# Expert mixtures: the second tile of a switch arm fetched inside the arm, and a code hint for the arm

## The chip, the cores and the metric

The kernel runs on one core of a Trainium2 chip. Its time is the device time of one execution in microseconds (us), the median of several runs. A core has five engines, each with an instruction queue of its own: PE (matrix products), DVE (vector), ACT (activations), POOL (here above all indirect DMAs and small tensor work) and SP (here the issuer of plain DMAs). They wait for each other through semaphores.

## The reference

The kernel computes twelve layers of a network on 1024 tokens of 256 numbers, float32 throughout: four groups (L0 to L3) of a cross-attention, an attention and a feed-forward layer. Three of the feed-forward layers, L0, L2 and L3, are mixtures of eight experts: a gate picks two experts per token (one in L2), and the token's output is the sum of the chosen experts' outputs, weighted by the gate. L3's in short:

```python
logits = x_flat @ router_w.T
probs = jax.nn.softmax(logits, axis=-1)
top_v, top_i = jax.lax.top_k(probs, K)             # K = 2 of E = 8
top_v = top_v / jnp.sum(top_v, axis=-1, keepdims=True)
...
h = jax.nn.gelu(jnp.einsum('ech,ehf->ecf', expert_in, w1), approximate=False)
y = jnp.einsum('ecf,efh->ech', h, w2)
...
out = out + tok * (gate * keep.astype(x.dtype))[:, None]
```

L2 has the same shape with biases and one expert per token; L0 has a gated hidden layer (silu(x W1) times x W2, then W3) of 682 units.

## The kernel before

The layers run one after the other. The change touches only the three mixtures, which share the function `experts` (L1647 to L1727).

Tokens are sorted by expert into tiles of 128 rows; a tile belongs to one expert. How many tiles each expert needs depends on the data. `slots` (L1571 to L1645) works this out on DVE, POOL and PE: `rows` (L1600, where each tile's expert lies in the weight table), `used` (L1602, how many tiles there are), then, by a chain over L1605, L1607, V (L1616 to L1624) and matmuls with R, `token` (L1642, the token of each row of each tile) and `share` (L1644, its gate). With 23 tiles at most in L0 and L3 and 15 in L2, `sure = tiles - 7` of them (16, 8, 16) are there whatever the data. These are written out straight. The remaining 0 to 7 are the business of a switch: `count`, the value of `used`, is loaded into a register of each engine, and each engine branches to the arm written for this number of further tiles. At the head of each arm an instruction hints at the branch out of it; the branch into it has no hint.

A tile i (`tile`, L1692) is:

- `fetch` (L1655): SP loads the expert's row from `rest` (a copy of `rows`) into a register and issues two DMAs, the first and second layer's weights, into one of three buffers W;
- `gather` (L1664): POOL fetches the tile's 128 token rows by an indirect DMA, xs;
- `turn` (L1672): PE transposes xs (`pst`), DVE or ACT in turn copy it to xT;
- `hidden`: PE multiplies with the first layer (`p` in L0, `psh` in L2 and L3, both under the helper's line L199), ACT and DVE apply the activation to hT;
- `pso`: PE multiplies with the second layer, DVE scales with the gate into y (L1705), and POOL adds y into the output in memory with an indirect scatter (L1706). Each scatter waits until the one before it has landed.

The order within a tile is fixed: fetch and gather of tile i+2, hidden of i, turn of i+1, pso of i. The straight tiles run with `end = sure + 2`, so that tile `sure - 1` still fetches and gathers for tile `sure + 1`, the second tile of whichever arm comes:

```python
        for i in range(sure):
            tile(i, sure + 2)
        held = dict(W), list(xs), list(xT)
        for n in self.tc.Switch(count - sure, E):
```

What is held across the switch (two tiles' weights, one tile's rows and one transposed tile) belongs to every arm, and its buffers are not used again within an arm. So one weight buffer of the three is left for an arm's third and further tiles. `self.fixed` pins the order of PE's instructions and a few others as written; what is not pinned, the loads of registers among them, is placed by a scheduler.

Of the kernel before, what the change touches and what calls it, by code (L numbers as in the profile page):

```python
# [27 lines left out]
E = 8  # L28
# [148 lines left out]
class Net:  # L177
# [1469 lines left out]
    def experts(self, name, xin, slots, weights, width, cols, tiles, wp, sp, pst, pso, hidden):  # L1647

        nc = self.nc
        rows, token, share, used = slots  # L1650
        total = self.dram.tile([NTOK + SPARE, D], F32, tag=f"{name}o", name=f"{name}o")
        nc.sync.dma_start(total[:NTOK, :].rearrange("(t p) d -> p t d", p=P), self.x)
        nc.sync.dma_start(total[NTOK:, :], xin[NTOK:, :])

        def fetch(i, rows):  # L1655
            W = wp.tile([P, width], F32, tag="W", name="W", bufs=3)
            r = nc.values_load(
                rows[0:1, i : i + 1], [mybir.EngineType.SP], min_val=0, max_val=(E - 1) * P
            )
            for o in (slice(0, cols), slice(cols, width)):  # L1660
                nc.sync.dma_start(W[:, o], self.io[weights][bass.ds(r, P), o])
            return W

        def gather(i):  # L1664
            xs = sp.tile([P, D], F32, tag="xs", name="xs", bufs=3)
            nc.gpsimd.indirect_dma_start(
                xs, None, xin, bass.IndirectOffsetOnAxis(token[:, i : i + 1], 0),
                bounds_check=NTOK + SPARE - 1,
            )
            return xs  # L1670

        def turn(xs):  # L1672
            ps = self.psum(pst, [P, 2, P], "pst")
            for kc in range(2):
                self.tr(ps[:, kc, :], xs[:, kc * P : (kc + 1) * P])
            xT = sp.tile([P, 2, P], F32, tag="xT", name="xT")
            self.evac(xT, ps)
            return xT

        self.fixed = True  # L1680

        W, xs = {0: fetch(0, rows)}, [gather(0), gather(1)]
        rest = sp.tile([P, tiles], U32, tag="rest", name="rest", bufs=1)
        self.pinned(nc.gpsimd.tensor_copy(rest, rows))
        W[1] = fetch(1, rest)

        sure = tiles - (E - 1)
        count = nc.values_load(used[0:1, 0:1], min_val=sure, max_val=tiles)
        self.warm(7)
        xT = [turn(xs.pop(0))]  # L1690

        def tile(i, end):  # L1692
            if i + 2 < end:
                W[i + 2] = fetch(i + 2, rest)
                xs.append(gather(i + 2))
            hT = hidden(W[i], xT.pop())
            if i + 1 < end:
                xT.append(turn(xs.pop(0)))
            n = hT.shape[1]
            W2 = W.pop(i)[:, cols : cols + n * D].rearrange("p (c n) -> p c n", n=D)  # L1700
            po = self.psum(pso, [P, D], "pso")
            for c in range(n):
                self.mm(po, hT[:, c, :], W2[:, c, :], c == 0, c == n - 1)
            y = sp.tile([P, D], F32, tag="y", name="y")
            nc.vector.tensor_scalar(y, po, share[:, i : i + 1], None, ALU.mult)  # L1705
            nc.gpsimd.indirect_dma_start(  # L1706
                total, bass.IndirectOffsetOnAxis(token[:, i : i + 1], 0), y, None,
                bounds_check=NTOK + SPARE - 1, compute_op=ALU.add,
            )

        for i in range(sure):
            tile(i, sure + 2)
        held = dict(W), list(xs), list(xT)
        for n in self.tc.Switch(count - sure, E):
            W, xs, xT = dict(held[0]), list(held[1]), list(held[2])
            for i in range(sure, sure + n):
                tile(i, sure + n)
        if name != "l3":
            self.warm(14)
        self.fixed = False  # L1720
        for t in range(0, NT, 2):
            nc.sync.dma_start(
                self.x[:, t : t + 2, :],
                total[t * P : (t + 2) * P, :].rearrange("(t p) d -> p t d", p=P),
            )
        if name != "l3":
            self.ready_all()  # L1727
# [842 lines left out]
```

## Time and profile before

| what | us |
|---|---|
| median of 3 runs (lowest to highest) | 3158.01 (3157.7 to 3166.25) |
| the profiled execution, its own time | 3158.53 |
| its span, first to last instruction | 3156.8 |
| L0's tiles: first hidden matmul to the last y | 641.27 to 801.98 |
| L2's tiles | 2394.16 to 2480.52 |
| L3's tiles | 2981.68 to 3142.36 |

The mean granted clock of PE over the span is 0.974 of full speed. In the profiled execution 19, 11 and 20 tiles were in use, so the arms for 3, 3 and 4 further tiles ran.

A row of the timeline gives the start and the busy time of one or several like instructions, the engine, the line, the operation with what it writes and reads, and in brackets how long the engine had been idle before it and which event ended that. Lines such as L199 belong to helpers, so that the tile's name tells what is done. An indirect DMA on POOL shows the time that POOL needs to issue it, not its transfer. Loads of registers, branches and hints are in no row; they show as idle time.

### The profile page before, as it was taken

How to read it: one execution, taken by the hardware profiler on the slowest of the kernel's cores; microseconds unless marked ns; L12 is line 12 of the kernel's file. 1: busy time of each engine (PE TensorE's matmuls, PEld its weight loads, DVE VectorE, ACT ScalarE, POOL GpSimd, SP SyncE). 2: the span in 40 equal slices, each digit the busy share in tenths (PEclk: the TensorE clock that was granted, in tenths of full speed). 3: DMA queues.
4: the chain of work that ended last, by engine and by line, in shares of the span. 5: the costliest groups of instructions: out<-in, count | busy, mean ns of one | idle time of the engine just before them, and what ended most of it. 6: DMA issues, size and time to landing. Idle time of an engine off the chain costs nothing.

```text
span 3156.8 us, 66834 instructions
## 1 busy us (share of the span) xinstructions
PE 2972.9 (94%) x28271; PEld 2215.7 (70%) x28271; DVE 1244.5 (39%) x3346; ACT 1354.2 (43%) x2691; POOL 336.0 (11%) x495
## 2 busy tenths in 40 slices
PE   7999998899899999999998999999999888889896
PEld 5666665699566666666676767777768767678796
DVE  5888885422344444444446512112142100145200
ACT  5888885311233333333333522222242477753211
POOL 1000001232100000000002100000022211111132
PEclk9999999899999999999999999999999899998898
DMA  6343341198112121212149111111117355510395
GB/s 224 115 140 122 112 137 64 58 330 296 34 49 72 55 84 44 82 46 80 55 136 297 35 42 63 42 63 42 63 50 274 109 190 190 179 40 3 138 335 181
DMA packets 174620, 368.52 MB, mean 117 GB/s; under 512 B 12614, under 2 KB 141646, under 8 KB 163726
## 3 DMA queue, kind: packets, MB, share of 16 engines
q1 hardware_dynamic: 163390, 348.78, 32.3%
q0 software_dynamic: 9600, 13.11, 2.1%
q8 instruction: 230, 3.77, 0.5%
q10 hardware_dynamic: 1280, 1.88, 0.2%
q14 instruction: 120, 0.98, 0.1%
HBM read 349.45 MB, written 14.68 MB: 115 GB/s over the span
## 4 chain that ended last, share of the span: by engine, by line
PE 77%; DMA 8%; issue 4%; DVE 4%; ACT 3%; POOL 1%; SPq 0%; POOLq 0%; DVEq 0%; ACTq 0%
PE acc L199 18%; PE pss L199 16%; PE pst L199 14%; PE pst L203 7%; PE psk L199 6%; DMA l3o<-y,token 4%; PE pso L199 4%; PE ps L199 3%; PE s L199 3%; PE p L199 3%; DMA l0o<-y,token 1%; DMA xs<-l2i,token 1%; PE py L199 1%; PE po L199 1%; PE psh L199 1%
## 5 line engine op out<-in xcount | busy, mean ns | idle before, releaser
L199 PE MATMUL acc<-ctx,st 128*128 128x257 f32 (+1 forms) x1664 | 397.2, 383 | 0.0
L199 PE MATMUL pss<-qk,ctxT 128*128 128x512 f32 (+1 forms) x832 | 391.5, 596 | 0.7 <-DVE qk L678 0.7
L199 PEld LDWEIGHTS acc<-ctx,st 128*128 128x128 f32 (+1 forms) x1664 | 310.2, 190 | 94.5 <-issue 36.1
L504 DVE CUSTOM_DVE_ANT_0 Sx<-s,mneg 128x384 f32<-128x384 f32 (+1 forms) x512 | 264.2, 570 | 88.1 <-PE s L199 88.1
L694 DVE TENSOR_TENSOR top<-pss,top 128x512 f32<-128x512 f32 x192 | 132.7, 691 | 403.6 <-ACT st L689 403.5
L203 PE MATMUL pst<-cst,Sx 128*128 128x128 f32 (+1 forms) x1736 | 251.6, 283 | 16.3 <-ACT aT L1280 8.6
L718 ACT ACTIVATE st<-st 128x512 f32<-128x512 f32 (+1 forms) x208 | 130.6, 629 | 294.5 <-DVE st L717 294.5
L990 ACT ACTIVATE Pr<-pss 128x512 f32<-128x512 f32 (+1 forms) x512 | 219.9, 524 | 59.5 <-PE pss L199 58.0
L548 ACT ACTIVATE PT<-pst 128x384 f32<-128x384 f32 x512 | 215.1, 489 | 63.1 <-PE pst L203 62.0
L199 PEld LDWEIGHTS pss<-qk,ctxT 128*128 128x128 f32 (+1 forms) x832 | 155.3, 187 | 122.4 <-issue 105.7
L203 PEld LDWEIGHTS pst<-cst,Sx 128*128 128x128 f32 (+1 forms) x1736 | 186.1, 141 | 62.4 <-ACT PT L548 27.7
L689 ACT COPY st<-pss 128x512 f32<-128x512 f32 (+1 forms) x208 | 121.5, 584 | 203.5 <-PE pss L199 203.5
L199 PE MATMUL pst<-wst,ctxT 128*128 128x256 f32 (+1 forms) x832 | 183.4, 380 | 0.0
L199 PE MATMUL psk<-ctxT,wst 128*128 128x512 f32 (+1 forms) x512 | 181.8, 513 | 0.8 <-ACT qT L852 0.8
L318 POOL TENSOR_TENSOR rs<-mv,cst 128x1 f32<-128x1 f32 x80 | 17.4, 217 | 1449.8 <-DVE mv L314 1420.1
L199 PEld LDWEIGHTS pst<-wst,ctxT 128*128 128x128 f32 (+1 forms) x832 | 153.5, 186 | 25.9 <-issue 2.7
L199 PE MATMUL pso<-W,hT 128*128 128x256 f32 x724 | 164.5, 379 | 0.0
L199 PE MATMUL pss<-q,ctxT 32*128 32x128 f32 (+1 forms) x3328 | 147.5, 293 | 16.6 <-issue 13.4
L199 PEld LDWEIGHTS psk<-ctxT,wst 128*128 128x128 f32 x512 | 88.3, 190 | 93.7 <-issue 92.1
L892 DVE TENSOR_TENSOR v<-pst,bvec 128x512 f32<-128x512 f32 (+1 forms) x112 | 73.1, 653 | 204.4 <-PE pst L199 204.4
L523 ACT ACTIVATE Sx<-Sx,neg 128x384 f32<-128x384 f32 (+1 forms) x256 | 145.8, 621 | 11.5 <-DVE neg L514 11.4
L199 PEld LDWEIGHTS pss<-q,ctxT 32*128 32x128 f32 (+1 forms) x3328 | 116.0, 188 | 47.7 <-issue 38.1
(404 smaller groups left out, 4427.1 us busy)
## 6 DMA issues: line engine op xcount, KB each, us to landing
ctxT<-in_ctxT_dram SPq DMA_DIRECT2D x64, 1601.0 KB
W<-in_L_experts_dram SPq DMA_DIRECT2D x51, 1024.0 KB
ctx<-in_ctx_dram SPq DMA_DIRECT2D x32, 1536.0 KB
W<-in_L_experts_dram SPq DMA_DIRECT2D x19, 1536.0 KB
ctx<-in_ctx_ones_dram SPq DMA_DIRECT2D x16, 1632.0 KB
ctx<-in_ctx_one_dram SPq DMA_DIRECT2D x16, 1542.0 KB
W<-in_L_experts_dram SPq DMA_DIRECT2D x19, 768.0 KB
W<-in_L_experts_dram SPq DMA_DIRECT2D x11, 1028.0 KB
```

The lines of the kernel that those rows point to most:

```text
L199: self.pinned(self.nc.tensor.matmul(out, lhsT, rhs, start=start, stop=stop))
L203: self.pinned(self.nc.tensor.transpose(out, in_, self.ident[:n, :n]))
L318: nc.gpsimd.tensor_tensor(rs[:, 0:1], mv[:, 1:2], self.c("eps"), ALU.add)
L504: self.pinned(nc.vector.tensor_tensor_reduce(out=Sx[:, j, :n], in0=ps[j][:, :n], in1=st["mneg"][:, o : o + n], op0=ALU.add, op1=ALU.max, s ...
L523: self.pinned(nc.scalar.activation(Sj[j], Sj[j], AF.Identity, bias=st["neg"][:, j - 2 : j - 1]))
L548: self.pinned(nc.scalar.activation(PT, ps, AF.Exp))
L689: pin(nc.scalar.copy(st[:kn], ps[:kn]))
L694: pin(nc.vector.tensor_tensor(top[b][:kn], ps[:kn], top[b][:kn], ALU.max))
L718: pin(nc.scalar.activation(st, st, AF.Exp, scale=HD**-0.5))
L892: nc.vector.tensor_tensor(o, ps[:kn, :n, :], bv[:kn].to_broadcast([kn, n, D]), ALU.add)
L990: nc.scalar.activation(st["Pr"][:kn, g : g + n, j, :], ps[j][:kn, :n, :], AF.Silu)
```

## The change

The straight tiles now run with `end = sure + 1`: the last of them fetches nothing, and weights and rows of tile `sure + 1` are asked for at the head of each arm that has at least two tiles, by the new function `ahead`. Across the switch one tile's weights and its transposed rows are held. Second, the loaded count less `sure` is put into a dictionary of one register expression per engine (`arm`), a hint for the switch is written after tile `sure - 3`, and the switch takes the same dictionary and the hint's label. The hint is not pinned: in the changed program the scheduler places the register load, the target's arithmetic and the hint ahead of the first tile of a stage, on DVE between L1605 and L1607, on POOL ahead of L1620, on ACT ahead of the first xT. On PE the load stays where it was and the hint follows just ahead of the first `pst` (in L2 somewhat earlier). On SP they stand ahead of the first fetch, in L2 after the fetch of tile 7. On POOL the gather of tile `sure + 1` now follows the scatter of tile `sure - 1`, in the arm; before, it preceded the last three scatters.

```diff
--- before.py
+++ after.py
@@ -1687,14 +1687,20 @@
         sure = tiles - (E - 1)
         count = nc.values_load(used[0:1, 0:1], min_val=sure, max_val=tiles)
         self.warm(7)
+        arm = {e: count - sure for e in count.engines} if hasattr(count, "engines") else {
+            e: count - sure for e in self.nc.engines
+        }
         xT = [turn(xs.pop(0))]
+
+        def ahead(i):
+            W[i] = fetch(i, rest)
+            xs.append(gather(i))
 
         def tile(i, end):
             if i + 2 < end:
-                W[i + 2] = fetch(i + 2, rest)
-                xs.append(gather(i + 2))
+                ahead(i + 2)
             hT = hidden(W[i], xT.pop())
-            if i + 1 < end:
+            if xs:
                 xT.append(turn(xs.pop(0)))
             n = hT.shape[1]
             W2 = W.pop(i)[:, cols : cols + n * D].rearrange("p (c n) -> p c n", n=D)
@@ -1709,10 +1715,14 @@
             )
 
         for i in range(sure):
-            tile(i, sure + 2)
+            tile(i, sure + 1)
+            if i == sure - 3:
+                self.tc.switch_hint(arm, E, label=name)
         held = dict(W), list(xs), list(xT)
-        for n in self.tc.Switch(count - sure, E):
+        for n in self.tc.Switch(arm, E, hint=name):
             W, xs, xT = dict(held[0]), list(held[1]), list(held[2])
+            if n > 1:
+                ahead(sure + 1)
             for i in range(sure, sure + n):
                 tile(i, sure + n)
         if name != "l3":
```

## The prediction

> **What bounds the kernel now.** The page comes first. Its chain that ended last puts 77% of the span on TensorE (PE), and the tiles of the three expert stages follow each other on PE at 8.17 us (L0), 7.25 us (L2) and 7.24 us (L3).
>
> ```profile
> PE 77%; DMA 8%; issue 4%; DVE 4%; ACT 3%; POOL 1%; SPq 0%; POOLq 0%; DVEq 0%; ACTq 0%
> ```
>
> So the change is worth what it takes from or adds to PE's idle time around the three switches. I read these in the timeline, 40 us at each switch. The tiles used were 19, 11 and 20, of which 16, 8 and 16 are sure, so the arms taken are n = 3, 3 and 4. L0:
>
> ```profile
> 774.50 0.48 DVE L1705 TENSOR_SCALAR y<-pso,share 128x256 f32<-128x256 f32 x1 [2.18 <-PE pso L199]
> 776.94 5.60 PE L199 MATMUL p<-xT,W 128*128 128x128 f32 x48 [2.48 <-SPq L1714]
> 777.90 1.55 POOL L1706 DMA_INDIRECT l0o<-y,token  x1 [4.82 <-DMA l0o<-y,token]
> 787.15 1.08 POOL L1666 DMA_INDIRECT xs<-l0i,token  x1 [7.69 <-PE p L199]
> ...
> 802.04 1.13 PE L199 MATMUL pso<-cst 128*128 128x256 f32 x4 [0.58 <-DVE y L1705]
> ```
>
> PE idles 2.48 us on entering the arm. On leaving it (last line), where a hint stands at the head of the arm, it idles 0.58 us, for DVE's y. POOL issues the last sure tile's scatter at 777.90, held by the scatter before, and its first gather of the arm 7.69 us after that scatter ends. L2 and L3:
>
> ```profile
> 2453.77 0.48 DVE L1705 TENSOR_SCALAR y<-pso,share 128x256 f32<-128x256 f32 x1 [6.76 <-PE pso L199]
> 2456.62 3.81 PE L199 MATMUL psh<-xT,W 128*128 128x128 f32 x32 [2.90 <-issue]
> 2458.55 1.55 POOL L1706 DMA_INDIRECT l2o<-y,token  x1 [6.27 <-DMA l2o<-y,token]
> 2466.18 1.09 POOL L1666 DMA_INDIRECT xs<-l2i,token  x1 [6.08 <-PE psh L199]
> 2469.11 0.41 PE L203 MATMUL pst<-cst,xs 128*128 128x128 f32 x2 [1.43 <-DMA xs<-l2i,token]
> ```
> ```profile
> 3103.04 5.44 PE L199 MATMUL psh<-xT,W 128*128 128x128 f32 x32 [4.04 <-issue]
> 3103.23 1.55 POOL L1706 DMA_INDIRECT l3o<-y,token  x1 [6.25 <-DMA l3o<-y,token]
> 3110.55 1.08 POOL L1666 DMA_INDIRECT xs<-l3i,token  x1 [5.77 <-DMA xs<-l3i,token]
> 3131.74 6.65 PE L199 MATMUL psh<-xT,W 128*128 128x128 f32 x32 [5.10 <-DMA W<-in_L_experts_dram]
> ```
>
> The same pattern, and in L3 one wait more: the fourth tile of the arm waits 5.10 us for its weights, because tiles 18 and 19 are fetched into one buffer. After the two long gaps of L3 the 32 hidden matmuls take 5.44 and 6.65 us instead of 3.73. The table of windows says why: the granted clock (third number from the end of a row) fell there, not after L2's 2.90 us gap.
>
> ```profile
> 2454.00:2473.00 19.00, 14.95 (x102) 13.99 (x103) 1.16 (x3) 4.82 (x17) 4.21 (x3) 1.00 0.54 158
> 3099.00:3112.00 13.00, 8.96 (x51) 8.58 (x52) 0.48 (x1) 1.46 (x3) 2.63 (x2) 0.87 0.60 192
> 3127.00:3142.00 15.00, 10.10 (x48) 9.37 (x48) 0.28 (x2) 1.19 (x2) 1.56 (x1) 0.77 0.45 152
> ```
>
> How long a gather takes from issue to landing is in the answer for the tile xs (least, median, most):
>
> ```profile
> DMA to landing us min/median/max: 2.9/4.7/7.0
> ```
>
> **The change part by part.** Losses before, to be set off. L0: gap 2.48. L2: gap 2.90, and the tile from 2463.94 to 2472.81 is 8.87 instead of 7.25 for the late gather: 1.62; 4.5 together. L3: gap 4.04, slow matmuls 1.71, weight wait 5.10, slow matmuls 2.92: 13.8.
>
> *The weights.* The fetch of tile `sure+1` moves from the last sure tile into the arm. It waits for the buffer of tile `sure-2`. SP has nothing between the fetch of tile `sure` (issued one tile, 7.2 to 8.2 us, earlier) and the arm, so even an unhinted entry of 6 us is hidden and it costs 0. The cover gone, it would be late microsecond for microsecond. Two buffers now serve within the arm: the weights of L3's tile 19 go where tile 17's were and start a tile earlier. Their first half takes 5.1 us (the wait above), tile 18 takes 7.24: the 5.10 and the 2.92 behind it go. L0 and L2 with n = 3 never had this wait.
>
> *The hint on PE.* The entry gap of 2.48, 2.90 and 4.04 becomes at most what the hinted exit shows, 0.58; I take 0.4.
>
> *The gather of tile `sure+1`*, moved with the weights, decides. Before, POOL issued it two tiles ahead, three scatters before the switch. Now it is in the arm, and on POOL's queue it stands behind the scatters of the last three sure tiles and the branch. The last of these is issued 2.9 to 4.3 us after its y, because each scatter waits for the one before to land. PE runs in order: it needs this gather for `pst`, ahead of the first arm tile's `pso`. PE reaches `pst` at the end of the last sure tile (774.46, 2453.73, 3099.00) plus 0.4 plus the hidden matmuls (5.35, 3.57, 3.57): 780.2, 2457.7, 3103.0. POOL ends the scatter at 779.45, 2460.10, 3104.78. Between neighbouring DMAs it idles 0.30; with branch and register work I take 0.8: gather issued at 780.25, 2460.9, 3105.6. Landing takes 2.9 (queue empty) to 4.7 (median, right behind a scatter). The Trainium skill, "DMA: Bandwidth & Descriptors", section "Queues, rings and completion order", says that a DMA engine takes turns between queues but consumes one queue's ring in order (it says so of hardware-made descriptors; POOL's share one queue too). By that rule the gather cannot pass the scatter issued 2.4 us earlier, and 4.7 is nearer; I take 4.2. The empty-queue row alone would make the sum about 4 us less. Landing: 784.5, 2465.1, 3109.8. Stalls of PE: 4.3, 7.4, 6.8 us.
>
> *The clock after these stalls.* Gaps of 2.48 and 2.90 left it full; 4.04 and 5.10 cost 1.71 and 2.92. The skill's "TensorE: Matmul & The Clock Gate", Part 1, gives a free-running window of about 3.4 us idle to slow and as long busy to recover, at half rate: up to 1.7 us a stall, and it speaks against this change. By the rule the three stalls would cost up to 5.1; by the rows I take 1.0 (L0, just past the edge), 2.5, 2.5: 6.0.
>
> *Early register loads.* The hint needs the tile count on every engine, so its load goes, with the target's arithmetic and the hint, from in front of the switch up into `slots` (all three stay ahead of the first tile on PE, ACT, DVE and POOL, not three tiles before the arm; on SP too, but for L2). ACT and POOL wait 17 us and 15 to 19 us there: 0. On PE the load stood there already. On SP it delays the first weights by some 0.2 us; PE waits then for the first xT: 0. If POOL's load ran past V's input, each stage would pay the excess, up to 1 us. On DVE it lies in the chain to `token`, right after L1605. No row has it; SP's load of `rows` bounds it above: written at 2968.96, DMA issued at 2970.08, 1.1 us with the issue. Below, 0.1, since it overlaps L1605. I take 0.4 a stage, 1.2 in all.
>
> Sum: L0 0.4+4.3+1.0-2.5 = +3.2; L2 0.4+7.4+2.5-4.5 = +5.8; L3 0.4+6.8+2.5-13.8 = -4.1; loads +1.2; together +6. The profiled execution took 3158.5 us (span 3156.8), 0.5 above the median of 3158.0, so 3164.
>
> **The rivals.**
> *Slower: POOL still pays for the arm's code.* From the scatter's end to the first gather POOL spent 7.70, 6.08 and 5.77 us. Less some 1 us for the load that moves away, 6.7, 5.1, 4.8 stay if the hint does not bring in POOL's code (it stands a stage ahead, and is not what PE's exit row tests). The gather then lands alone, 2.9 later: 789.1, 2468.1, 3112.5, which is 4.6, 3.0 and 2.7 later than above, plus some 1.5 for L0's clock: +18, 3176. It decides once POOL's entry takes over about 2 us, the lead that the scatter's landing gives anyway. For it: POOL's gaps are the longest of all engines. Against: the hinted exit on PE.
> *No change: the gather does not queue behind the scatter* and lands in 2.9: stalls 2.9, 6.1, 5.5, clock 0, 1.7, 1.7: 0.8+3.7-6.2+1.2, about 0: 3158. For it: the scatter's data are half landed by then. Against: the median of 4.7.
> *Faster: the gather is in time.* Only the gaps and L3's weights count: -2.1-4.1-13.4+1.2 = -18, 3140. It needs the last scatter about 5 us earlier in all three stages, and the rows show it held by the scatter before.
> *The change does nothing to entry*: if no hint works, PE's gap stays but hides under the gather, which is the first rival again.
>
> **How the numbers follow.** About 0.3% (9.5 us) is what a measurement of this kernel tells from no change. My forecast (3159 to 3170) has 0.58, its upper tail beyond 9.5 us a quarter of that; the slow rival 0.27, nearly all beyond; no change 0.10; faster 0.05. Slower: 0.15+0.26, about 0.41; faster 0.05; the same 0.54. Range: from 4 us below, for the early landing and a cheap load, to 20 above, for the slow rival: 3154 to 3178. The likeliest case's own range is 3159 to 3170.
>
> **What would show it.** In the changed profile's chain of waits: PE `pst` waits for DMA xs after the first hidden matmuls of each arm, 3 to 8 us; PE's entry gap under 0.6; no wait for W in L3's arm; in the timeline POOL's first gather of each arm within 1 us of the scatter's end (5 or more means the slow rival); the granted clock below 1 after the stalls in L2 and L3; DVE idle 0.3 to 0.6 between L1605 and L1607. I am wrong if PE meets no gather wait in the arms, or if L3's W wait is still there.

## The result and the profile after

The changed kernel takes 3174.74 us (median of 15 runs, 3166.69 to 3180.4), against 3157.72 of the kernel before in runs on the same chip (15 runs, 3151.49 to 3171.17). The two medians are 17 us apart; the ratio as it was estimated from all these runs is 1.0038, 95% interval 1.0026 to 1.005: slower by 0.38%, or 12 us, more than the 0.3% that a measurement of this kernel can tell from no change. The profiled execution took 3171.95 us, with a span of 3170.2 (3156.8 before) and a mean granted clock of 0.968 (0.974).

The page's chain that ended last is of no use this time. It follows POOL's scatters back into L3's arm and stops there; the line by engines reads

```profile
DMA 1%; issue 0%; POOL 0%; POOLq 0%
```

where that of before ran through the whole span. So I go to the timeline at once, with the same stretches as before. First L0's switch. The columns are start, busy time, engine, line, operation, and in brackets the engine's idle time before and what ended it.

```profile
778.68 5.52 PE L199 MATMUL p<-xT,W 128*128 128x128 f32 x48
778.88 0.48 DVE L1711 TENSOR_SCALAR y<-pso,share 128x256 f32<-128x256 f32 x1 [2.18 <-PE pso L199]
...
781.03 1.55 POOL L1712 DMA_INDIRECT l0o<-y,token  x1 [6.22 <-DMA l0o<-y,token]
...
783.03 1.09 POOL L1666 DMA_INDIRECT xs<-l0i,token  x1 [0.46 <-PE p L199]
...
789.12 0.69 PE L203 MATMUL pst<-cst,xs 128*128 128x128 f32 x2 [4.91 <-DMA xs<-l0i,token]
789.60 5.04 PE L199 MATMUL pso<-W,hT 128*128 128x256 f32 x12
...
811.33 0.92 PE L199 MATMUL pso<-cst 128*128 128x256 f32 x3 [0.58 <-DVE y L1711]
```

TensorE (PE) enters the arm without a gap: the first line has no bracket, where before it had 2.48. POOL issues its first gather 0.46 us after the scatter. But PE then stands 4.91 us before the transpose of that gather's rows, and the `pso` behind it takes 5.04 us instead of 2.76. L2, then L3:

```profile
2469.26 1.55 POOL L1712 DMA_INDIRECT l2o<-y,token  x1 [7.24 <-issue]
2471.44 1.09 POOL L1666 DMA_INDIRECT xs<-l2i,token  x1 [0.63 <-issue]
...
2475.76 0.66 PE L203 MATMUL pst<-cst,xs 128*128 128x128 f32 x2 [8.27 <-DMA xs<-l2i,token]
...
2476.21 5.69 PE L199 MATMUL pso<-W,hT 128*128 128x256 f32 x16
```
```profile
3118.30 1.55 POOL L1712 DMA_INDIRECT l3o<-y,token  x1 [5.89 <-issue]
...
3124.76 1.09 POOL L1666 DMA_INDIRECT xs<-l3i,token  x1 [4.91 <-DMA l3o<-y,token]
...
3127.66 0.69 PE L203 MATMUL pst<-cst,xs 128*128 128x128 f32 x2 [7.90 <-DMA xs<-l3i,token]
...
3128.14 5.70 PE L199 MATMUL pso<-W,hT 128*128 128x256 f32 x16
...
3133.68 3.73 PE L199 MATMUL psh<-xT,W 128*128 128x128 f32 x32
```

The same stall, 8.27 and 7.90 us, and after it 5.7 us for sixteen `pso` matmuls that take 3.62 at full clock. The table of windows shows the granted clock (third number from the end) down in all three places, L0, L2 and L3:

```profile
779.00:794.00 15.00, 10.09 (x60) 9.00 (x59) 1.48 (x3) 1.35 (x3) 3.69 (x3) 0.78 0.55 188
2470.00:2482.00 12.00, 6.24 (x21) 5.25 (x22) 0.00 (x1) 0.37 (x1) 2.95 (x3) 0.57 0.31 94
3120.00:3134.00 14.00, 6.34 (x21) 5.32 (x22) 0.07 (x1) 0.77 (x2) 3.16 (x3) 0.63 0.42 126
```

In L3 the fourth tile's wait for its weights (5.10 us before) is gone. All that was foreseen. What was not is in L0's `slots`, 150 us ahead of the switch:

```profile
627.76 0.29 DVE L1605 TENSOR_TENSOR place<-place,oh 128x128 f32<-128x128 f32 x1
...
629.37 0.29 DVE L1607 TENSOR_REDUCE slot<-place 128x16 f32<-128x128 f32 x1 [1.32 <-issue]
...
632.36 1.08 PE L199 MATMUL pst<-V,R 128*128 128x69 f32 x8 [1.90 <-DVE V L1623]
...
633.76 3.48 PE L199 MATMUL pst<-V,R 128*128 128x69 f32 x16
...
639.83 0.18 DVE L1639 TENSOR_SCALAR none<-pst 128x23 f32<-128x23 f32 x1 [3.57 <-PE pst L199]
```

and the rows of the kernel before that answer to the DVE and the matmul rows:

```profile
627.95 0.29 DVE L1605 TENSOR_TENSOR place<-place,oh 128x128 f32<-128x128 f32 x1
...
628.27 0.29 DVE L1607 TENSOR_REDUCE slot<-place 128x16 f32<-128x128 f32 x1
...
631.26 1.08 PE L199 MATMUL pst<-V,R 128*128 128x69 f32 x8 [0.30 <-DVE V L1623]
...
632.66 1.90 PE L199 MATMUL pst<-V,R 128*128 128x69 f32 x16
```

DVE stands 1.32 us between L1605 and L1607, where the early register load is (before, 0.03). PE's gap before the first V,R matmul grows from 0.30 to 1.90, and 1.4 us later PE runs at half speed: sixteen matmuls take 3.48 us instead of 1.90.

To add this up I cut each stage in two. *Slots* is the time from the start of L1605 to the first transpose of an xs; *tiles* from there to the start of the last y. Six numbers describe a kernel, and hardly anything outside them is touched by the change:

| | L0 slots | tiles | L2 slots | tiles | L3 slots | tiles | sum |
|---|---|---|---|---|---|---|---|
| before | 12.20 | 161.35 | 13.07 | 87.03 | 11.64 | 161.33 | 446.6 |
| after | 16.32 | 166.72 | 13.70 | 94.41 | 12.36 | 158.88 | 462.4 |
| difference | +4.12 | +5.37 | +0.63 | +7.38 | +0.72 | -2.45 | +15.8 |

The span grew by 13.4, so code that the change does not touch was 2.4 us faster in this execution. That part differs from one execution to the next: a second profiled execution of the changed kernel (below) has 462.7 us in the six pieces and a span of 3181.3, so 10.8 us more elsewhere. The pieces, not the spans, are compared from here on.

### The profile page after: what moved, and what is told of

Read it like the earlier page. It is cut to its first block, busy times and chain, and to the rows that moved or that the text cites. A ratio compares the mean times of both kernels' runs of the same rounds, so it can differ in the third digit from the quotient of the medians.

```text
span 3170.2 us, 66922 instructions
## 1 busy us (share of the span) xinstructions
PE 2983.8 (94%) x28271; PEld 2226.2 (70%) x28271; DVE 1244.3 (39%) x3346; ACT 1355.5 (43%) x2691; POOL 336.6 (11%) x495
## 3 DMA queue, kind: packets, MB, share of 16 engines
q8 instruction: 227, 3.72, 0.5%
## 5 line engine op out<-in xcount | busy, mean ns | idle before, releaser
L199 PE MATMUL pso<-W,hT 128*128 128x256 f32 x724 | 171.0, 390 | 0.0
L199 PEld LDWEIGHTS pso<-W,hT 128*128 128x128 f32 x724 | 138.5, 197 | 18.0
```

The costliest lines, as they stand in the source:

```text
L199: self.pinned(self.nc.tensor.matmul(out, lhsT, rhs, start=start, stop=stop))
```

## The experiments

Two theories were to be told apart. Mine: the change wins at the branch (hint) and at L3's weights, loses more by the gather that it moves behind the last scatter, and loses again in `slots` by the loads that the hint needs early. The rival: the slots' loss has another cause, or the lateness of the gather is the branch itself, so that hint and move can't be judged apart.

**hint_only.** The hint alone: the fetch of tile `sure + 1` goes back ahead of the switch.

```diff
...
-            tile(i, sure + 1)
+            tile(i, sure + 2)
...
-            if n > 1:
-                ahead(sure + 1)
```

> Keeps the hint of the change, puts the fetch of tile sure+1 (weights and gather) back ahead of the Switch, as in the kernel before. My theory: the hint has two effects. It costs in the slots: DVE's register load sits in the chain that makes the tokens, about +4 us in L0 (1.3 of load, the rest TensorE at half clock behind the opened gap), +0.6 and +0.7 in L2 and L3, together +5.3, so the first tile's transpose starts about 11.9 us after L0's place product (L1605 to first xs transpose) against 12.2 of before plus 4. It gains at the branch: PE's entry gaps of before (2.48, 2.90, 4.04) shrink to 0.5 or less and the half-clock losses behind them go (1.6 and 1.7): about -11. The weight wait of L3 (5.1 plus 2.9 at half clock) stays. Sum -6 against before: 3152. Rival A (the slots' delay in the changed kernel came from something other than the early loads): first transposes as before and 3147. Rival B (the hint does nothing for TensorE, the entry was only hidden by the moved fetch): entry gaps stay at 2.5 to 4, time 3163.

Measured: 0.9974 of before (0.996 to 0.9988), about 8 us faster. The pieces: slots 16.33, 13.16, 12.39; tiles 159.09, 92.47, 155.28. PE's entry gaps are gone in all three stages, L3's weight wait is there:

```profile
3146.94 1.41 PE L199 MATMUL psh<-xT,W 128*128 128x128 f32 x5 [5.11 <-DMA W<-in_L_experts_dram]
```

So the hint does what it says, and brings its own loss in the slots. Rivals A and B fall. The pieces sum to +2.1 against before, not to the -8 of the medians. L2 stands out: there a gather came 7.11 us late, behind scatters that waited long for each other. The profiled execution (3172.63 us) was the slowest of this kernel's 22, so I take all its runs (0.9974) for the whole and the rows for the mechanism.

**move_only.** The move alone, the switch without a hint: `self.tc.Switch(count - sure, E)` and no `switch_hint`.

> Keeps the move of the fetch into the arm, takes the hint out. My theory: the slots are as in before (0), but POOL and TensorE enter their arm as late as in before (POOL sat 5.8 to 7.7 us idle there), and now the gather of tile sure+1 is behind that entry: in L0 and L2 its landing is about 5 us later than in the changed kernel, so the stall of TensorE before that transpose is about 10 and 13 us, in L3 (where POOL's entry was already 4.9 with the hint) about 9. Sum against before: L0 +10.5, L2 +12.5, L3 -1: 3180. Rival (the gather's lateness is the queue behind the scatter alone, the entry is overlapped with it): stalls of 4.9, 8.3 and 7.9 as in the changed kernel and, without the loads in the slots, 3168.

Measured: 1.0012 (0.9997 to 1.0027), some 4 us above before (the medians are 6 us apart). I had +22 and the rival +10: neither number came, and the rival's is the nearer. (The median of 3168.47 looks like the rival's 3168, but in these runs the kernel before took 3162.51.) The slots are those of before (12.17, 13.07, 11.73). L2's switch:

```profile
2466.73 6.30 PE L199 MATMUL psh<-xT,W 128*128 128x128 f32 x32 [4.46 <-issue]
2467.59 1.55 POOL L1712 DMA_INDIRECT l2o<-y,token  x1 [6.56 <-PE psh L199]
...
2473.12 1.09 POOL L1666 DMA_INDIRECT xs<-l2i,token  x1 [3.98 <-PE psh L199]
...
2476.18 0.66 PE L203 MATMUL pst<-cst,xs 128*128 128x128 f32 x2 [3.15 <-DMA xs<-l2i,token]
```

PE loses 4.46 on entry and then 3.15 on the gather, 7.6 together, against 8.27 in the changed kernel. L0 has 2.85 + 4.57, L3 3.99 + 2.31. Over the three stages this is 21.3 us, against 21.1 of stalls in the changed kernel (4.91, 8.27, 7.90). So the gap at the branch and the stall behind it are for the most part one wait for the same gather: what the hint takes from the first, the second takes back (L0's 2.5 us excepted). I had counted them twice, although the prediction's last rival says that the gap "stays but hides under the gather". For the changed kernel this means that its hint buys TensorE little at the switch. What it saves is rather the half clock after the gap (the first row's 6.30 us are 3.73 at full clock). In the pieces the tiles are 6.3 us better with the hint (420.0 against 426.3) and the slots 5.4 us worse (42.4 against 37.0).

So hint and move do not add. Against before, the hint alone is worth -8 us, the move alone +4, and both together are +11 to +12, not -4: once the gather is moved, the hint costs some 7 to 8 us, by intervals that just touch. The pieces of single executions have it about even there (462.4 against 463.3). Which of the two is nearer no run here settles.

**weights_hint.** One part of the change put back: the gather of tile `sure + 1` ahead of the switch, its weights in the arm.

```diff
-        def tile(i, end):
+        def tile(i, end, more=0):
             if i + 2 < end:
                 ahead(i + 2)
+            elif i + 2 < end + more:
+                xs.append(gather(i + 2))
...
-            tile(i, sure + 1)
+            tile(i, sure + 1, 1)
...
             if n > 1:
-                ahead(sure + 1)
+                W[sure + 1] = fetch(sure + 1, rest)
```

> The changed kernel with one part put back: the gather of tile sure+1 is issued ahead of the Switch as in before, its weights are fetched inside the arm, the hint stays. My theory: the stall on the gather (4.9, 8.3, 7.9 us, and about 2.1 each at half clock behind it) goes, but the weights' fetch that hid behind it comes out: issued at the arm's entry, 2.1 to 2.4 MB[...] are 7 to 8 us, against some 4 us of TensorE work until they are needed, so a wait on W of 2 to 4 us in each stage. Slots +5.3 as in the changed kernel. Sum against before: +5.3, L0 -2.1+3.5, L2 -4.1+3, L3 -12+3.5: about -4, 3154; -20 against the changed kernel. Rival (the weights are covered in the arm as the prediction's zero for their move says): no wait on W, 3144. Rival (the stall was not the gather): TensorE still waits 5 to 8 us before the second transpose, 3174 as the changed kernel.

Measured: 0.9947 (0.9923 to 0.9971), about 17 us faster than before and some 28 faster than the changed kernel (0.9947 against 1.0038). Slots 16.69, 13.12, 12.34 as in the changed kernel; tiles 158.69, 83.60, 148.30. In L0 the tiles go through the switch at the even pace of 8.17 us:

```profile
769.73 5.52 PE L199 MATMUL p<-xT,W 128*128 128x128 f32 x48
...
777.89 5.52 PE L199 MATMUL p<-xT,W 128*128 128x128 f32 x48
...
786.06 5.52 PE L199 MATMUL p<-xT,W 128*128 128x128 f32 x48
```

No stall on a gather above 0.3 us and no wait on W in any of the three arms. The stall was the gather, and the prediction's zero for the weights was right; my later fear of 2 to 4 us was wrong, since I counted half a tile between the fetch and its use where it is a whole one, 7.2 to 8.2 us.

**late.** The changed kernel, but DVE, ACT and POOL load the count from a copy that needs the tokens first, and so cannot be placed ahead of them.

```diff
+        late = small.tile([P, 1], U32, tag="late", name="late")
+        nc.vector.scalar_tensor_tensor(
+            late, share[:, :1], 0.0, end[:, E - 1 : E], ALU.mult, ALU.add
+        )
...
+        count = nc.values_load(used[0:1, 0:1], early, min_val=sure, max_val=tiles)
+        after = nc.values_load(late[0:1, 0:1], later, min_val=sure, max_val=tiles)
...
+        arm = {e: count - sure for e in early}
+        arm.update({e: after - sure for e in later})
```

> The changed kernel, but DVE, ACT and POOL load the tile count from a copy that is made after the tokens (SP and PE from the old one, as before), so that their register loads and hints come after the slots' chain and not inside it. My theory: the slots' chain is back at the times of before (first transpose 12.2 us after the place product in L0 against 16.3 in the changed kernel; TensorE's granted clock there back at 0.95 from 0.65), so -5 against the changed kernel: +11 against before, 3169. If only the direct load counts (1.3, 0.7, 0.7) and the clock's loss has another cause: -2.5, 3172. Rival (POOL's long entry in L3, 4.9 us, came from the hint being too early, 130 us ahead): it stays in this run, since the hint is only 5 us later.

Measured: 1.0009 (0.9994 to 1.0025), 8 to 9 us better than the changed kernel. Slots 12.21, 12.85, 11.97: those of before but for 0.1 us, so nearly all of the 5.5 us is back. The sixteen V,R matmuls take 1.90 us again:

```profile
631.79 1.08 PE L199 MATMUL pst<-V,R 128*128 128x69 f32 x8 [0.87 <-DVE V L1623]
...
633.20 1.90 PE L199 MATMUL pst<-V,R 128*128 128x69 f32 x16
```

POOL's long entry in L3 stays (5.42 us), and the stalls too (4.59, 7.75, 9.03).

**late_dve.** The same with DVE's load alone made late.

> The changed kernel with only DVE's load of the tile count after the tokens; ACT and POOL load early, as in the changed kernel. If DVE alone carries the slots' loss: place product to first transpose 12.2, 12.9 and 12.0 us as in the run with all three late. If POOL's early load ahead of its V product costs too: up to 1 us more. The tiles behind are as in the changed kernel: 166.7, 94, 159.

Measured in a single execution: slots 12.23, 12.88, 11.97. DVE carries the whole loss of the slots; the early loads on ACT and POOL cost nothing there, as the prediction had it.

**fill.** Four more filler matmuls on PE ahead of L0's V,R matmuls (`self.warm(9)` became `self.warm(13)` there).

> The changed kernel with four more filler matmuls of 128x256 on TensorE ahead of L0's slot matmuls (and nothing else). My theory: of the 4.1 us that L0's slots lost, 1.3 is DVE's load and 2.7 is TensorE at half clock, since the load opened a gap of 1.9 us ahead of the first V,R matmul. With the gap filled the clock stays up: place product to first transpose 13.6 to 14.0 us against 16.3 in the changed kernel and 12.2 before; granted clock over the V,R matmuls back to about 0.95 from 0.65. Time -2.5 against the changed kernel. Rival (the slow matmuls wait for something else, the fetch of W or the loads themselves): 16.3 stays, or worse by the fillers' 2 us.

Measured: 1.0024 (1.001 to 1.0038), L0's slots 16.17. It did not test what it should: the trace has as many filler matmuls ahead of L0's V,R matmuls as that of the changed kernel (28), so that none was gained, and PE's gap was 2.36 us, wider than the 1.90 there.

**fill_held.** The same again, with fillers that read the place product and so stay behind L1605:

```diff
+        if K == 2:
+            heat = self.psum(self.heat[0], [P, D], self.heat[1])
+            for _ in range(9):
+                self.mm(heat, place.rearrange("p g e -> p (g e)"), self.cst[:, :D])
         ps = self.psum(pp, [P, 3, tiles], "pst")
```

> The filler once more, now so that it cannot be taken elsewhere: nine filler matmuls of 128x256 that read the place product, so that TensorE runs from there to the first V,R matmul in L0 and L3; DVE's load stays in the chain. My theory (load plus clock): place product to first transpose in L0 13.5 to 14.0 us against 16.3 in the changed kernel and 12.2 before; the sixteen V,R matmuls of the middle 1.9 us instead of 3.5. Rival (they are slow for another reason than TensorE's idle gap): 16 us stays.

Measured in a single execution: L0's slots 13.22 (3160.42 us in all).

```profile
627.26 4.12 PE L199 MATMUL pso<-cst,place 128*128 128x256 f32 x18 [0.45 <-DVE place L1605]
631.42 1.97 PE L199 MATMUL pst<-V,R 128*128 128x69 f32 x16
...
634.00 1.90 PE L199 MATMUL pst<-V,R 128*128 128x69 f32 x16
```

DVE's load is still in the chain (1.32 us of idle time before L1607), but PE has no gap before the V,R matmuls and runs them at full speed. So of the 4.12 us, 1.0 is left with the load alone (13.22 against 12.20) and 3.1 were the clock. (By the changed kernel's own rows it is 1.3 and 2.8.)

These two runs have the changed kernel's hint, and in L2 PE's entry gap was there all the same: 3.72 us in fill and 1.89 in fill_held, where the other runs with a hint have none. So a hint does not bring TensorE in without a gap every time; why not, no run here shows.

**hint_late and weights_late.** What the runs so far leave standing: the kernel before with the hint and late loads, and the same with the weights (but not the gather) moved into the arm.

> The kernel before with only the hint, its loads on DVE, ACT and POOL after the tokens. Expected: slots 12.2, 12.9, 12.0; tiles 159.1, 86 or less, 155.3: about -8 to -10 against before, so 0.997. The weight wait of L3 (5.1 us) stays: between this run and the one with the weights in the arm the difference is L3's wait with its half-clock stretch, 7 us. Rival (the early hint is what makes it work): no gain, entry gaps as before.

> Weights of tile sure+1 fetched inside the arm, its gather ahead of the Switch, hint kept, and the loads of DVE, ACT and POOL after the tokens: what the experiments so far leave standing. Expected from the segments: slots of L0, L2, L3 at 12.2, 12.9, 12.0 us (as in the run with late loads) and tiles at 158.7, 83.6, 148.3 (as in the run with weights alone moved): 427.7 against 446.6 in the kernel before, so -19, about 0.994, and -35 against the changed kernel. Rival (a late hint comes too late or collides with the first gathers): entry gaps of 2.5 us or more return, -11.

Measured: hint_late 0.9953 (0.9935 to 0.9971), pieces 12.13, 157.67, 13.37, 83.07, 12.09, 156.31, sum 434.6; weights_late 0.9934 (0.9909 to 0.996), 3142.35 us against 3163.05 of before in the same runs, pieces 12.24, 157.69, 12.87, 84.34, 12.11, 150.43, sum 429.7. The second beats both kernels, the one before by 0.66% and the changed one by about 1.0% (0.9934 against 1.0034 of the next run). A hint placed late works on PE as well as an early one; POOL comes into L3's arm 4.2 us after its scatter even so, and PE waits 2.16 us for a gather there. Between the two, L3's weights are worth 5.9 us in the pieces; in the medians the two intervals overlap.

**after_again.** The changed kernel once more, beside these.

> The changed kernel once more, beside the others on one chip: 1.0038 of before again (1.0026 to 1.005), stalls on the moved gather of about 5, 8 and 8 us, L0's place product to first transpose at 16.3 us. Rival (POOL's long entry in L3, 4.9 us, was a chance of one execution): an entry below 1 us there, the stall in L3 down to about 5.

Measured: 1.0034 (1.002 to 1.0047); L0's slots 16.36; stalls 4.61, 9.39 and 9.45; POOL's entry in L3 5.39. The loss in the slots, the stalls and POOL's entry are no chance of one execution.

## Where the prediction was right and where not

The sign was right and so was the order of events, but the likeliest time, 3164, was +6 where +12 was measured. It was the prediction's whole range that held the median of 3174.7; the likeliest case's own range ended at 3170. The whole range reached that far up for the slow rival, which was at work in one stage of three, so that it held the result was in part luck. And it gave "the same", within 9.5 us, a chance of 0.54 and slower one of 0.41, where slower came. Term by term, by the profiled executions:

| term | predicted | measured |
|---|---|---|
| PE's entry gaps of the arms | 1.2 | 0 |
| stalls on the moved gather | 4.3, 7.4, 6.8 | 4.91, 8.27, 7.90 |
| half clock after the stalls | 1.0, 2.5, 2.5 | 2.3, 2.1, 2.1 |
| losses that go | -20.8 | all gone: -20.8 |
| early register loads, with what follows | 0.4, 0.4, 0.4 | 4.12, 0.63, 0.72 |
| first tile's hidden matmuls | 0 | 0.5, 1.4, 1.2 |
| sum | +6 | +15.3 of 15.8 |

*The step that failed* is "Early register loads": "On DVE it lies in the chain to `token`, right after L1605 ... I take 0.4 a stage, 1.2 in all", with 1.1 as the upper bound. It was in the right place and too small twice over. The load itself took 1.29 us in L0 (1.32 of idle time against 0.03), above the bound, and 0.6 to 0.7 in L2 and L3. I had bounded it by SP's load of another value, which is another engine. The Trainium skill, "Runtime: NRT & Kernel Launch", section "The launch sequence", has about 1.3 us for register loads, there from HBM at launch; as an upper end that price would have held here. But that is a load of other words from another memory, so its nearness to 1.29 may be chance. The larger part is what the load opened: PE's fillers in `slots` are counted so that PE stays busy just until V is ready, and 1.3 us more on DVE left it idle for 1.9. A cost on a chain was priced as its own length; the price was its length plus the clock of the engine that waits at the chain's end. late_dve and fill_held show both halves.

*The gather* was the main loss, as predicted, and weights_hint shows it by taking it away. The stalls were 2.6 us longer in sum, for different reasons. In L0 POOL entered within 0.5 us as foreseen, but the gather took 6.1 us to land (783.03 to 789.12) where I took 4.2. What held it can be read from the scatter issued before it: that one took 7.7 us to land (781.03 to 788.7), and the gather was there right behind it; in L2 likewise, the scatter at 2475.3 (2469.26 and 6.0 us) and PE's transpose of the gather's rows at 2475.76. So the gather did not pass the scatter, as the prediction had it, but the scatter's own landing was the term to price. The section of the Trainium skill that it names for this ("Queues, rings and completion order") gives the order in which descriptors are taken up, and adds that a later one may finish its write before an earlier one; "cannot pass" was more than it says. In L3 it landed in 2.9, but POOL entered 4.91 us late where I took 0.8. So the slower rival's mechanism, POOL not coming into the arm in time, was at work in L3 alone. Its cause stays open. POOL's idle time before its first gather of L3's arm was 4.91 and 5.39 us in the changed kernel, 5.42 in late, 5.40 and 5.64 in late_dve and fill_held (POOL's own load early), 2.78 in fill, 4.22 without a hint, and 4.44 and 4.24 in hint_late and weights_late; in hint_only and weights_hint it was 0.73. So neither the place of the hint nor that of the gather decides alone: the wait was short only where POOL's hint stood early and the gather of tile `sure + 1` stayed ahead of the switch. It is about as long as the landing of the scatter before (7.2 us from its issue in the changed kernel, where the gather came 6.46 after it, so not simply that), and about as long as an entry without a hint.

*The clock after the stalls*: 6.4 in sum against 6.0, though I took too little for L0 and too much for the others. *The first tiles* ran their first hidden matmuls 0.5 to 1.4 us slower than before. The granted clock explains the size: these matmuls ran at half clock for 4.7, 2.8 and 2.4 us before (L0, L2, L3) and for 5.7, 5.8 and 5.0 us after, and half of each difference is 0.5, 1.5 and 1.3. When the clock comes back depends on a grid of time (last section). The time scatters between executions (in L2 5.0 to 6.6 us over the kernels here), and I put it down to no part of the change; so some 3 of the 15.8 us may be this execution's chance.

*The weights*: zero, as said, and L3's wait gone. *ACT, POOL and SP loads*: zero, as said. *The rivals*: "no change" and "faster" both needed an early gather, which did not come. *The signs to look for*: the gather's stalls, PE's entries and the missing W wait were as listed; "DVE idle 0.3 to 0.6 between L1605 and L1607" was contradicted by 1.32, and that row alone would have led to the rest.

## What to carry to other kernels

A hint or any early register load is placed where a scheduler finds room by its own prices, and here that was in the middle of the chain that the next stage waits for; give it an input that exists only after that chain. A gap taken away at a branch is worth only what no later wait takes back: here the hint gained 8 us alone and lost 7 to 8 beside the moved gather, so two changes at one place want to be timed apart and together. When a fetch is moved past a branch, ask for each of its DMAs what it comes to stand behind on its queue: here the weights could move for nothing on SP, while the gather, on POOL, went behind the last scatter. And where fillers keep an engine's clock up, they are cut to the length of the wait they cover, so a delay of one microsecond upstream can cost four.

## What the runs showed of the hardware

The granted clock fell after a shorter gap than I had expected. Ahead of L0's V,R matmuls PE's gap was 0.30 (before), 0.87 (late) and 1.05 us (weights_late), and the sixteen matmuls behind took 1.90 us each time; with a gap of 1.90 to 1.92 (after, hint_only, after_again) they took 3.48 to 3.52, and with 2.36 (fill) 3.32. The slow stretch began only with the second group of matmuls, some 1.4 us after work had resumed.

The traces show why. In all twelve the granted clock is either full or half, and it changes only at the lines of a grid of 3.41 us, the same through a whole trace. The Trainium skill, "TensorE: Matmul & The Clock Gate", Part 1, has such a free-running window, of about 3.4 us, and half clock after an idle one. The window here was not idle. These are the windows of the grid around L0's V,R matmuls in the changed kernel (length, busy time of PE, ..., granted clock as the third number from the end):

```profile
626.96:630.37 3.41, 3.11 (x14) 2.18 (x12) 1.99 (x12) 0.00 (x0) 0.00 (x0) 1.00 0.00 0
630.37:633.79 3.42, 1.52 (x12) 1.41 (x12) 3.02 (x6) 0.00 (x0) 1.09 (x1) 1.00 0.86 283
633.79:637.20 3.41, 3.41 (x18) 3.41 (x17) 1.07 (x2) 0.00 (x0) 0.00 (x0) 0.50 0.94 395
```

The gap of 1.90 us lay whole in the second of them and left PE busy for 44% of it; at its end the clock was halved. In late the window with the gap was busy for 2.55 of 3.42 us, 75%, and the clock stayed. Over all windows of the twelve traces at full clock, those with PE busy for less than 40% of the time were each followed by a window at half (139 of 139), those between 40 and 50% in 66 of 88 cases, and those above 50% in 92 of 8433. (Busy times of PE are modelled in part, so the edge is rough.) So it is not the length of the gap that counts but what it leaves of its window; by this a gap of 1.9 us cut in two by a line of the grid would have left the clock up, which no run here shows. Coming back takes more than leaving: of the windows at half clock none busy for less than 75% was followed by full clock (0 of 142), and of those above 95% some were not either (84 of 341).

A register load between two DVE instructions cost some 1.3 us in L0 and 0.6 to 0.7 in L2 and L3, in both profiled executions of the changed kernel and in hint_only, weights_hint and fill. Why L0's is twice as long no run here shows.
